# Zero fills and bands issued from SyncE, eight units of image 0 first, weights loaded one at a time, and a later second half of the reciprocal spread

## The chip, the cores and the metric

The kernel runs on one core of one Trainium2 chip. The metric is the device time in microseconds of one execution; the runs before the change took 3051.0, 3051.75 and 3055.79 us.

The engines are called as the profile calls them: PE (TensorE) with its weight loads PEld, DVE (VectorE), ACT (ScalarE), POOL (GpSimd), and SP (SyncE), which here only issues DMAs.

## The reference, cut to what matters

Two images of 256 channels and 64 x 64 pixels, all float32, pass two layers.

Layer 0 is attention over all 4096 pixels of an image, 8 heads of 32 channels: q, k and v are 1x1 convolutions, `softmax(q k / sqrt(32)) v` is concatenated to x and goes through a 1x1 convolution, and a mask resized from 32 x 32 blends the result with x.

Layer 1 multiplies by a channel gate (two small matmuls, sigmoid), does attention in windows of 8 x 8 pixels with 4 heads, adds, shuffles the channels, and ends with a spatial gate: two grouped 7 x 7 convolutions with batch norm between and after, and `x * sigmoid(y)`.

```
attn = softmax(einsum('bnd,bmd->bnm', q, k))
hybrid = conv1x1(concat([x, attn @ v]), Wf, bf);  x = hybrid*m + x*(1-m)
x = x * sigmoid(channel gate);  x = x + window_attention(x)
y = relu(bn1(conv7x7(x, sa_w1)));  y = bn2(conv7x7(y, sa_w2));  out = x * sigmoid(y)
```

## The kernel before, in words

**Preparation.** q, k and v of all pixels are computed and stored in DRAM. `prepare` readies the small tensors, among them a DRAM tile of zeros (`zero_s`) and the scaled filter rows `r1_s` and `r2_s`, from which the banded weight matrices of the 7 x 7 convolutions are made.

**Bands.** The convolutions run on PE as products with banded matrices, one per unit (`NU` = 16 units of four groups of channels), 896 KB each, in the DRAM tensor `w_s`. `bands()` is a generator that makes them by DMAs alone: 16 copies of `zero_s` into `w_s` (L341, DRAM to DRAM), then 156 copies that put filter rows on the diagonals (L349, L355, L362), each for all 16 units at once in pieces of 28 or 7 floats. Every `next` on it issues one DMA, and the loop calls it in every fifth slot (`i % 5 == 1`).

**The main loop.** It has 1024 slots: 2 images x 8 chunks of 512 queries x 2 head groups x 32 blocks of 128 keys; 64 slots make a chunk. Slot i computes the scores of slot i+2 on PE (`sa`, L632), whose exponentials go through ACT into one of `EB` = 8 buffers `ea` (L642), and the products of slot i with v (`ava`, L661). DVE adds the exponentials up for the denominators (`suma`, L663). Every four slots `load_piece` fetches k and v of a later piece (L559, L561) on SP, 256 KB each, into three buffers of each kind; such a load waits until PE is done with the piece whose buffer it takes[...].

**After a chunk.** Actions are queued with a delay in slots by `at`: `denominators` (`dna`) at DN = 8 slots after the chunk's last, the reciprocal one later, then `spread(0)` and `spread(1)` (`rda`, L699, each with an ACT copy, L706), the multiplication of `f` on DVE (L716), and the appending of `stage(b, c)`. `stage` is a generator with the rest of layers 0 and 1 for the chunk, from `hya` (L731) to the output projection `opa` (L952) and the addition into `xo` (L963), whose rows go to the DRAM tensor `x_s` (L978). It advances by one step in every fourth slot (`i % 4 == 0`), 13 calls in all.

**The convolutions** stand in another generator, `convolve`. It goes through `items`: a unit with image 0 alone, with image 1 alone, or with both. Units below `EARLY` are first done for image 0 alone, whose rows are all in DRAM by then. Item k is `conv1(k)` (`c1a`, L1043), `conv2(k)` (`c2a`, L1067) and `gate(k)` (`za`, L1089), which also stores the output (L1102); while item k is worked on, `conv1(k + 1)` goes ahead of `conv2(k)`. Each step ends in a `yield`. In the last chunk the loop starts the generator (first rows and unit 0's weights are loaded), and behind the last slot its steps are put between the steps of the last stage. When this stage is done, `staged` is set, and the rest of the items run alone: `more` gives out four tiles `xla` for rows of both images and loads the next four items' rows, which wait until the last `xs<-xo` stores have landed.

The weights of a unit (`wa<-ws`, L1015, 896 KB on SP) take the `e` buffers, of which there are 8. Units 1 to 8 are loaded at the generator's start, and the others, kept in `again`, one by one when a unit's buffer is free:

```
            for u in range(1, 1 + EB):
                load_w(u)
...
                if xcs or k + 4 < EARLY:
                    load_rows(k + 4)
                if (u >= 2) == (B - 1 in images) and u and again:
                    load_w(again.popleft())
```

Between `staged` and item `EARLY` the gates store on POOL alone; later on POOL and SP by turns.

Of the kernel before, what the change touches and what calls it, by code (L numbers as in the profile page):

```python
# [17 lines left out]
B, C, H, W = 2, 256, 64, 64  # L18
# [11 lines left out]
AHEAD = 2  # L30
EB = 8
DN = 8
EARLY = 7
HEADS1, HD1 = 4, 64
WS = 8
NW = W // WS
# [10 lines left out]
NU = NG // UG  # L47
# [8 lines left out]
def conv_seq_kernel(ctx: ExitStack, tc: tile.TileContext, a, out):  # L56
    nc = tc.nc
# [13 lines left out]
    def psum2(name):  # L71
        return ps["pair"].tile([P, 2, CH], F32, tag="s", name=name)
# [53 lines left out]
    w_s = dram.tile([NU, P, 2 * 32 * UW], F32, name="ws")  # L126
# [33 lines left out]
    zero_s = dram.tile([P, 2 * 32 * UW], F32, name="zeros")  # L160
# [171 lines left out]
    def spread(row, n):  # L332
        f = row.shape[-1]
        return row.rearrange("p u f -> u p f").to_broadcast([NU, n, f])


    def bands():
        band1 = w_s.rearrange("u p (m f) -> u (p m) f", f=UW)
        band2 = w_s.rearrange("u p (m f) -> u (p m) f", f=UW // 4)
        for u in range(NU):  # L340
            nc.gpsimd.dma_start(w_s[u], zero_s)  # L341
            yield
        for q in range(4):
            for dy in range(KS):
                r0, r1 = max(0, dy - PAD), min(RB, RB + dy - PAD)
                p0, m0, n = 32 * q + 1 + r0, 1 + r0 - dy + PAD, r1 - r0
                k = KS * q + dy
                at0, step = p0 * 64 + m0, 64 + 1
                nc.gpsimd.dma_start(  # L349
                    band1[:, at0 : at0 + step * (n - 1) + 1 : step, :], spread(r1_s[k : k + 1], n)  # L350
                )
                yield
                for i in range(4):
                    at0, step = p0 * 256 + 128 + i * 32 + m0, 256 + 1
                    nc.gpsimd.dma_start(  # L355
                        band2[:, at0 : at0 + step * (n - 1) + 1 : step, :],
                        spread(r2_s[k : k + 1, :, i], n),
                    )
                    yield
            for i in range(4):  # L360
                at0 = 32 * q * 256 + 128 + i * 32 + 1
                nc.gpsimd.dma_start(  # L362
                    band2[:, at0 : at0 + RB, :], spread(r2_s[32 + q : 33 + q, :, i], RB)
                )
                yield
# [157 lines left out]
    def pipeline(arm, shifted, pools):  # L523
# [23 lines left out]
        stages = deque()  # L547

        def at(delay, action):
            later.append((now[0] + delay, action))  # L550
# [99 lines left out]
        def products(i):  # L650
            b, c, g, m = slots[i]
            if m == 0:
                acc[0] = avp.tile([P, CH], F32, tag="av", name=f"av{arm}_{i}")
                acc[1] = ep.tile([P, HG, CH], F32, tag="sum", name=f"sum{arm}_{i}", bufs=3)
                totals[b, c, g] = acc[1]
            av, total = acc[0], acc[1]
            e, v = es[i], vts[b, c, g, m // PB]
            start, stop = m == 0, m == NMB - 1
            for j in range(HG):
                r = slice(32 * j, 32 * j + 32)  # L660
                nc.tensor.matmul(av[r, :], v[:, m % PB, r], e[:, j, :], start=start, stop=stop)  # L661
            if m > 0:
                nc.vector.tensor_add(total, first[0] if m == 1 else total, e)  # L663
            e = es.pop(i)
            if start:
                first[0] = e
            if stop:
                if g == 0:
                    fts[b, c] = fp.tile([P, KC, CH], F32, tag="f", name=f"f{arm}_{b}_{c}")
                f = fts[b, c]  # L670
                nc.scalar.copy(f[:, g, :], av)  # L671
                if g == 0:
                    return
                both = [totals.pop((b, c, gg)) for gg in range(KC)]
                inv = fp.tile([P, P], F32, tag="inv", name=f"inv{arm}_{i}")
                rd = fp.tile([P, KC, 4, P], F32, tag="rd", name=f"rd{arm}_{i}")


                def denominators():
                    s = psum2(f"dn{arm}_{i}")  # L680
                    for h in range(HEADS0):
                        for q in range(4):
                            r = slice(32 * q, 32 * q + 32)
                            nc.tensor.matmul(
                                s[r, 0, 0:P],
                                keysum[:, h].rearrange("p i h -> p (i h)"),
                                both[h // HG][:, h % HG, q * P : (q + 1) * P],
                                start=(h == 0),
                                stop=(h == HEADS0 - 1),
                            )  # L690
                    nc.scalar.copy(inv, s[:, 0, 0:P])


                def spread(hh):
                    t = psum2(f"rd{arm}_{i}_{hh}")
                    for gg in range(KC):
                        for q in range(2):
                            r = slice(64 * hh + 32 * q, 64 * hh + 32 * q + 32)
                            nc.tensor.matmul(  # L699
                                t[:, q, gg * P : gg * P + P],  # L700
                                spread_h[r, gg].rearrange("p j d -> p (j d)"),
                                inv[r, :],
                                start=True,
                                stop=True,
                            )
                    nc.scalar.copy(  # L706
                        rd[:, :, 2 * hh : 2 * hh + 2, :],
                        t[:, :, 0 : KC * P].rearrange("p q (g n) -> p g q n", g=KC),
                    )


                at(DN, denominators)
                at(DN + 1, lambda: nc.vector.reciprocal(inv, inv))
                at(DN + 2, lambda: spread(0))
                at(DN + 3, lambda: spread(1))
                at(DN + 4, lambda: nc.vector.tensor_mul(f, f, rd.rearrange("p g q n -> p g (q n)")))  # L716

# [271 lines left out]
        def convolve():  # L991
# [8 lines left out]
                nc.gpsimd.memset(t, 0.0)  # L1000
                ycs.append(t)
            xs, ws, ys = {}, {}, {}
            again = deque([*range(1 + EB, NU), 1])
            dst = out.rearrange("b (g i) r w -> b i r g w", i=4)

            def load_w(u):
                if u >= NU:
                    return
                n = 2 * 32 * UW
                if u == 0:  # L1010
                    t = cpool.tile([P, n], F32, name=f"w{arm}{u}")
                else:
                    t = ep.tile([P, HG, CH], F32, tag="e", name=f"w{arm}{u}")
                    t = t.rearrange("p h n -> p (h n)")[:, 0:n]
                nc.sync.dma_start(t, w_s[u])  # L1015
                ws[u] = t
# [103 lines left out]
            load_rows(3)  # L1120
            load_w(0)
            pool = yield
            for u in range(1, 1 + EB):
                load_w(u)
            conv1(0)
            yield
            for k, (u, images) in enumerate(items):
                while len(xs) <= k + 1 < len(items):
                    if not more():
                        yield  # L1130
                conv1(k + 1)
                yield
                more()
                z = conv2(k)
                yield
                more()
                gate(k, z)
                if xcs or k + 4 < EARLY:
                    load_rows(k + 4)

                if (u >= 2) == (B - 1 in images) and u and again:
                    load_w(again.popleft())

        def run_later():
            for _ in range(len(later)):
# [22 lines left out]
        for i, (b, c, g, m) in enumerate(slots):  # L1168
            now[0] = i
            if (b, c, g, m) == (B - 1, NCHUNK - 1, 0, 0):  # L1170
                for _ in banded:
                    pass
                conv = convolve()
                next(conv)
            if m % PB == 0:
                load_piece(i // PB + AHEAD)
            if g == KC - 1 and m == 0:
                nxt = (b, c + 1) if c + 1 < NCHUNK else (b + 1, 0)
                if nxt[0] < B:
                    load_q(*nxt)  # L1180
            rest = scores(i + 2) if i + 2 < len(slots) else None
            products(i)
            if rest:
                rest()
            if g == KC - 1 and m == NMB - 1:
                at(DN + 5, lambda b=b, c=c: stages.append(stage(b, c)))
            run_later()
            if i % 5 == 1:
                next(banded, None)
            if i % 4 == 0:  # L1190
                run_stages()
# [102 lines left out]
```

## Time and profile before

| what | value |
|---|---|
| median of 3 runs | 3051.75 us (3051.0 to 3055.79) |
| the profiled execution's own time | 3062.01 us |
| its span | 3060.2 us |
| mean granted PE clock | 0.987 |
| PE, DVE, ACT, POOL busy | 97%, 82%, 81%, 12% |
| DMA moved | 266.02 MB, mean 87 GB/s |

The profile is of one execution, which took 10 us more than the median run. Times in it count from the span's start. Some landmarks: the loop's first scores run at 187 us, the last ones at 2823 us, PE's last matmul ends near 3043 us. A row of a timeline gives the start, the time it takes, the engine, the line of the source, the operation, the tiles written and read, the number of instructions merged, and in brackets how long the engine stood idle before it and what ended this. "SPq" is SP's queue of DMA issues.

### The profile page before, as it was taken

How to read it: one execution, taken by the hardware profiler on the slowest of the kernel's cores; microseconds unless marked ns; L12 is line 12 of the kernel's file. 1: busy time of each engine (PE TensorE's matmuls, PEld its weight loads, DVE VectorE, ACT ScalarE, POOL GpSimd, SP SyncE). 2: the span in 40 equal slices, each digit the busy share in tenths (PEclk: the TensorE clock that was granted, in tenths of full speed). 3: DMA queues.
4: the chain of work that ended last, by engine and by line, in shares of the span. 5: the costliest groups of instructions: out<-in, count | busy, mean ns of one | idle time of the engine just before them, and what ended most of it. 6: DMA issues, size and time to landing. Idle time of an engine off the chain costs nothing.

```text
span 3060.2 us, 60785 instructions
## 1 busy us (share of the span) xinstructions
PE 2967.3 (97%) x25114; PEld 1005.6 (33%) x25114; DVE 2498.5 (82%) x1347; ACT 2478.7 (81%) x4147; POOL 369.4 (12%) x636
## 2 busy tenths in 40 slices
PE   9968989999999999999999999999999999999897
PEld 3541222222322222232222232322222322223675
DVE  3227989899989999899999898999999898999211
ACT  5537969898989899898989898989898898988333
POOL 8020000101010101010100101010101000000256
PEclk9988999999999999999999999999999999999999
DMA  8574212424252424243322314242424232423364
GB/s 241 200 248 106 63 52 60 71 63 73 60 78 60 70 70 73 67 66 75 63 65 64 68 60 73 62 71 60 69 71 71 66 71 66 102 63 101 96 208 112
DMA packets 155999, 266.02 MB, mean 87 GB/s; under 512 B 43016, under 2 KB 61756, under 8 KB 155456
## 3 DMA queue, kind: packets, MB, share of 16 engines
q1 hardware_dynamic: 127424, 213.86, 25.3%
q0 software_dynamic: 23728, 45.48, 9.8%
q8 instruction: 200, 3.28, 0.5%
q10 hardware_dynamic: 4560, 2.70, 0.3%
q14 instruction: 87, 0.71, 0.1%
HBM read 213.49 MB, written 66.13 MB: 91 GB/s over the span
## 4 chain that ended last, share of the span: by engine, by line
PE 71%; DVE 13%; DMA 4%; issue 2%; ACT 2%; POOL 1%; SPq 0%; DVEq 0%; ACTq 0%
PE sa L632 29%; PE ava L661 27%; DVE suma L663 11%; PE qka L802 4%; PE hya L731 4%; DMA ka<-ks 2%; PE vwa L888 2%; ACT ea L642 1%; PE opa L952 1%; PE c2a L1067 1%; POOL out_dram L1102 1%; DMA wa<-ws 1%; PE c1a L1043 1%; PE sca L836 1%; PE rda L699 1%
## 5 line engine op out<-in xcount | busy, mean ns | idle before, releaser
L663 DVE TENSOR_TENSOR suma<-suma,ea 128x2048 f32<-128x2048 f32 x960 | 2198.7, 2290 | 122.7 <-ACT ea L642 39.5
L642 ACT ACTIVATE ea<-sa 128x512 f32<-128x512 f32 (+1 forms) x3072 | 2043.7, 745 | 122.0 <-PE sa L632 75.4
L632 PE MATMUL sa<-qa,ka 32*128 32x512 f32 x8192 | 1186.6, 641 | 39.7 <-DMA ka<-ks 38.2
L661 PE MATMUL ava<-ea,va 128*32 128x512 f32 x8192 | 1093.8, 605 | 0.3 <-ACT fa L671 0.3
L632 PEld LDWEIGHTS sa<-qa,ka 32*128 32x128 f32 x8192 | 331.2, 183 | 793.6 <-ACT ea L642 688.7
L661 PEld LDWEIGHTS ava<-ea,va 128*32 128x32 f32 x8192 | 161.8, 108 | 781.9 <-issue 755.7
L978 POOL DMA_DIRECT2D xs<-xo x94 | 66.1, 711 | 2302.4 <-DVE xo L963 2302.2
L1102 POOL DMA_DIRECT2D out_dram<-za x204 | 114.9, 571 | 102.4 <-DVE za L1089 55.5
L802 PE MATMUL qka<-ua,qkv_w 128*128 128x512 f32 x256 | 118.4, 605 | 0.0
L663 DVE TENSOR_TENSOR suma<-ea,ea 128x2048 f32<-128x2048 f32 x32 | 73.1, 2285 | 51.3 <-ACT ea L642 51.3
L1089 DVE TENSOR_TENSOR za<-za,xla 128x1536 f32<-128x1536 f32 (+1 forms) x16 | 22.6, 1409 | 110.0 <-ACT za L1083 56.7
L453 DVE TENSOR_REDUCE top<-sq 128x512 f32<-128x2048 f32 x16 | 36.6, 2286 | 81.4 <-ACT sq L447 81.4
L739 ACT ACTIVATE ta<-hya,bf 128x512 f32<-128x512 f32 x32 | 20.3, 684 | 99.7 <-PE hya L731 99.7
L1067 PE MATMUL c2a<-yca,wa 32*128 32x192 f32 (+1 forms) x1288 | 95.9, 440 | 4.0 <-issue 3.8
L1077 ACT ACTIVATE za<-c2a 128x384 f32<-128x384 f32 (+1 forms) x46 | 25.8, 615 | 86.3 <-DMA out_dram<-za 50.2
L743 DVE TENSOR_TENSOR ta<-ta,mca 128x512 f32<-128x512 f32 x32 | 22.0, 689 | 88.3 <-ACT ta L739 88.3
L1067 PEld LDWEIGHTS c2a<-yca,wa 32*128 32x128 f32 x1288 | 87.0, 314 | 14.9 <-issue 14.0
L857 ACT ACTIVATE ewa<-ewa,mxwa 128x64 f32<-128x64 f32 x256 | 85.5, 362 | 1.5 <-DVE mxwa L848 1.5
L355 POOL DMA_DIRECT2D ws<-r2s x112 | 69.7, 625 | 95.3 <-DMA ws<-r2s 48.6
L815 ACT ACTIVATE qka<-qka,qkv_b 128x512 f32<-128x512 f32 x64 | 40.7, 695 | 41.6 <-PE qka L802 41.6
L802 PEld LDWEIGHTS qka<-ua,qkv_w 128*128 128x128 f32 x256 | 46.0, 189 | 71.3 <-issue 58.7
L434 PE MATMUL q<-x,WqT 128*128 128x512 f32 x128 | 62.2, 631 | 5.6 <-DMA WqT<-in_WqT_dram 5.6
(141 smaller groups left out, 1620.5 us busy)
## 6 DMA issues: line engine op xcount, KB each, us to landing
ka<-ks SPq DMA_DIRECT2D x256, 256.0 KB
va<-vs SPq DMA_DIRECT2D x256, 256.0 KB
wa<-ws SPq DMA_DIRECT2D x17, 896.0 KB
ws<-zeros POOLq DMA_DIRECT2D x16, 896.0 KB, 23.9
xs<-xo POOLq DMA_DIRECT2D x78, 140.0 KB, 8.0
xla<-xs SPq DMA_DIRECT2D x25, 420.0 KB
x<-in_x_dram SPq DMA_DIRECT2D x16, 512.0 KB
qs<-qst SPq DMA_DIRECT2D x16, 512.0 KB
```

The costliest lines, as they stand in the source:

```text
L355: nc.gpsimd.dma_start(band2[:, at0 : at0 + step * (n - 1) + 1 : step, :], spread(r2_s[k : k + 1, :, i], n),)
L434: nc.tensor.matmul(s[:, g, :], w[:, kc, g * P : (g + 1) * P], rhs, start=(kc == 0), stop=(kc == KC - 1),)
L632: nc.tensor.matmul(heads[j], k[r, cols], q[r, g, :], start=True, stop=not shifted)
L642: nc.scalar.activation(e[:, h, :], tile, AF.Exp, scale=SCALE0)
L661: nc.tensor.matmul(av[r, :], v[:, m % PB, r], e[:, j, :], start=start, stop=stop)
L663: nc.vector.tensor_add(total, first[0] if m == 1 else total, e)
L731: nc.tensor.matmul(s[:, oc, :], wf[:, kc, oc * P : (oc + 1) * P], f[:, kc - KC, :] if half else xw[kc], start=(kc == 0), stop=(kc == 2 * K ...
L802: nc.tensor.matmul(s[:, j, :], wqkv[:, kc, o : o + P], u[:, kc, :], start=(kc == 0), stop=(kc == KC - 1),)
L857: nc.scalar.activation(e[:, n, :], e[:, n, :], AF.Exp, bias=mx[:, n : n + 1], accum_out=rs[:, n : n + 1],)
L978: eng.dma_start(x_s[b, n, p + r0 : p + r1].rearrange("r g w -> g r w"), xo[64 * h : 64 * h + 64, oc, r0 - WS * c : r1 - WS * c, :],)
L1067: nc.tensor.matmul(tiles[j // 2][:, j % 2, 0 : n * W], w[r, d], y[r, 0:n, d : d + W], start=(d == 0), stop=(d == KS - 1),)
L1102: engines[stores % len(engines)].dma_start(dst[b, i, r0:r1, UG * u : UG * u + UG, :], z[p + r0 : p + r1, :, nb * m + n, :],)
```

## The change

1. `bands()` issues its 16 zero fills and 156 band copies on SP instead of POOL. Their place in the program's order is the same.
2. `EARLY` is 8 instead of 7: unit 7 is done for image 0 alone and later for image 1 alone, where one item did both. There are 24 items instead of 23.
3. At the convolutions' start only units 1 and 2 are loaded. The others follow one at a time behind the gates, in every item but item 7.
4. `spread(1)` comes one slot later than before, and so do the multiplication of `f` and the appending of the stage.

```
-EARLY = 7
+EARLY = 8
...
         for u in range(NU):
-            nc.gpsimd.dma_start(w_s[u], zero_s)
+            nc.sync.dma_start(w_s[u], zero_s)
             yield
...
-                nc.gpsimd.dma_start(
+                nc.sync.dma_start(
                     band1[:, at0 : at0 + step * (n - 1) + 1 : step, :], spread(r1_s[k : k + 1], n)
                 )
...
-                    nc.gpsimd.dma_start(
+                    nc.sync.dma_start(
                         band2[:, at0 : at0 + step * (n - 1) + 1 : step, :],
...
-                nc.gpsimd.dma_start(
+                nc.sync.dma_start(
                     band2[:, at0 : at0 + RB, :], spread(r2_s[32 + q : 33 + q, :, i], RB)
                 )
...
                 at(DN + 2, lambda: spread(0))
-                at(DN + 3, lambda: spread(1))
-                at(DN + 4, lambda: nc.vector.tensor_mul(f, f, rd.rearrange("p g q n -> p g (q n)")))
+                at(DN + 4, lambda: spread(1))
+                at(DN + 5, lambda: nc.vector.tensor_mul(f, f, rd.rearrange("p g q n -> p g (q n)")))
...
-            again = deque([*range(1 + EB, NU), 1])
+            weights = deque([*range(1, NU), 1])
...
-            for u in range(1, 1 + EB):
-                load_w(u)
+            for _ in range(2):
+                load_w(weights.popleft())
...
-                if (u >= 2) == (B - 1 in images) and u and again:
-                    load_w(again.popleft())
+                if weights and (k < EARLY - 1 or k >= EARLY):
+                    load_w(weights.popleft())
...
-                at(DN + 5, lambda b=b, c=c: stages.append(stage(b, c)))
+                at(DN + 6, lambda b=b, c=c: stages.append(stage(b, c)))
```

## The prediction

> **What bounds the kernel now.** I read the page first, then the timelines of the two places where TensorE is not full. The page:
>
> ```profile
> span 3060.2 us, 60785 instructions
> PE 2967.3 (97%) x25114; PEld 1005.6 (33%) x25114; DVE 2498.5 (82%) x1347; ACT 2478.7 (81%) x4147; POOL 369.4 (12%) x636
> PE   9968989999999999999999999999999999999897
> DMA  8574212424252424243322314242424232423364
> L663 DVE TENSOR_TENSOR suma<-suma,ea 128x2048 f32<-128x2048 f32 x960 | 2198.7, 2290 | 122.7 <-ACT ea L642 39.5
> L632 PE MATMUL sa<-qa,ka 32*128 32x512 f32 x8192 | 1186.6, 641 | 39.7 <-DMA ka<-ks 38.2
> ```
>
> PE is full except in the third slice and in the last tenth. L632 waited 39.7 us in all, 38.2 of it for k tiles: nearly one wait. The windows, cut from one `hya` to the next, show the loop between (columns: window, its length, busy time of PE, PEld, DVE, ACT, POOL with counts, clock, DMA share, GB/s):
>
> ```profile
> 735.55:899.50 163.95, 163.43 (x1369) 47.70 (x1369) 151.83 (x79) 145.21 (x247) 13.62 (x21) 1.00 0.36 68
> 2369.32:2532.50 163.18, 162.44 (x1369) 47.43 (x1369) 151.06 (x78) 145.12 (x247) 5.74 (x8) 1.00 0.27 68
> ```
>
> A chunk lasts 163.2 to 164.0 us and PE works through it: 64 slots of 2.07 us (scores 1.07, products 1.00) plus some 30 us of stage matmuls. DVE has 151 us, so it is second. Little is to be had there. Now the third slice, by the timelines of POOL, SP and PE:
>
> ```profile
> 189.56 3.40 POOL L341 DMA_DIRECT2D ws<-zeros  x7 [0.19 <-issue]
> ...
> 216.09 0.49 POOL L341 DMA_DIRECT2D ws<-zeros  x1 [2.87 <-DMA ws<-zeros]
> ```
>
> ```profile
> 192.12 0.43 SPq L559 DMA_DIRECT2D ka<-ks  x1
> ```
>
> ```profile
> 202.32 1.06 PE L661 MATMUL ava<-ea,va 128*32 128x512 f32 x8
> 241.08 2.09 PE L632 MATMUL sa<-qa,ka 32*128 32x512 f32 x8 [37.69 <-DMA ka<-ks]
> ```
>
> The program spaces the zeros five slots apart, but POOL has nothing else to wait for and issues all 16 (14.7 MB) in 28 us. The k tile issued on SP at 192.12 lands 48.8 us later. PE stands for 37.69 us, then runs two slots at a lower clock. Last, the tail on PE:
>
> ```profile
> 2833.75 2.65 PE L1067 MATMUL c2a<-yca,wa 32*128 32x192 f32 x40
> 2840.19 1.68 PE L1067 MATMUL c2a<-yca,wa 32*128 32x192 f32 x16 [3.79 <-issue]
> ...
> 2900.84 3.56 PE L1067 MATMUL c2a<-yca,wa 32*128 32x192 f32 x56
> 2908.44 4.72 PE L1043 MATMUL c1a<-xla,wa 128*32 128x192 f32 x56 [4.04 <-DMA xla<-xs]
> ```
>
> Two gaps, one in mid-tile where no operand is awaited, one for the rows of image 1 to come back from DRAM. After 2908.44 PE has no gap until its last matmul near 3043.
>
> [...]
>
> **Zeros on SP.** SP meets each zero in program order, between k and v loads that wait for PE to free buffers. So zeros go out one per five slots (10.4 us). Their transfer is about 3.1 us each (16 in some 50 us of the flood, 314 GB/s in that window), plus 512 KB of k and v per four slots: half of what the DMA engines moved in the flood. Gone: the gap, 37.7 us, and the slow slots (241.08 to 248.13 is 7.05 us for two slots, 2.9 over 4.14): 40.6 us. Given back: the pause had let DVE catch up. DVE needs 2.39 us a slot against PE's 2.07; 57 slots after the pause (score groups stretch from 1.14 to 1.46 us at 359.79) the eight `e` buffers are full and PE goes at 2.39 until the first stage. Those 57 slots now begin 8 earlier: 8 x 0.32 = 2.6 us. **Net -38.0 us.**
>
> **Bands on SP.** 156 more issues. SP's own rows bound one: 0.32 us (k) to 0.69 us (`xs<-xo`, 1.37 for two, as many short pieces). With zeros at 0.43 that is 57 to 115 us of SP, which waits 2,100 us for PE on the lines of k and v. Queued behind them are those loads, on which PE waits. Their lead: k issued at 251.45 is needed in slot 18, near 268.8, so 17 us; v (256.58) is alike. On the ring a band weighs little: DMA share is 0.36 in the window with 13 bands, 0.27 in the one with none, 0.09 x 163 / 13 = 1.1 us each. I take 0 us; the bound above is the rival D below, below it is nothing, as no wait on bands is on PE. POOL keeps the row stores, which nobody on the path waits for in the loop.
>
> **Spread.** `spread(1)` and the multiply move one slot, and the stage append too, from DN+5 to DN+6. Stages are advanced only in slots divisible by four, and the append fell on slot 12, so the stage now begins at slot 16. Same matmuls, copies and DMAs; its x and mask loads move along, with 48 slots still ahead of use. All waits of `rda` for the reciprocal after the first chunk come to 7.0 us, and they are on `spread(0)`, which stays. Bounds: -7 us (all gone) and +12 us (15 chunks at 164.0 instead of 163.2). I take 0. The last step of the stage of (1,6) now falls behind the slots: 1.3 us of DVE and four POOL stores (2.8 us), under `hya`.
>
> **Tail.** (1) At its start SP issues 8 weight loads of 0.92 MB (2814 to 2832); now 2. [...] Gone: 3.8 us, and the slow clock behind it (`hya` 6.02 against 3.70, `rda` 2.02 against 1.36, c2a's rest 0.6): 3.4 us. Together -7 us; 0 if the reading is wrong. (2) Weights 3 to 6 now go behind the output stores and rows of gates 0 to 3, in place of arriving early. Such loads took 5.4 to 7.6 us in the chain; unit 3 is issued near 2854 and wanted near 2859 on the earlier clock, 5 and 6 similar, 4 has room: +2 us (0 to 5). (3) Unit 7 is issued after gate(4). In SP's order the four `xla` loads stand ahead, and they wait for the row stores (issued at 2904.72). So the added item of image 0, meant for that round trip, waits for it too: 4 x 0.43 MB + 0.92 MB = 2.64 MB at 300 GB/s is 8.8 us, plus 2 us of latency, from an issue near 2904.7 - 5 = 2899.7. Its conv1 starts near 2910.5; before, the item at that place started at 2908.4. So the gap grows from 4 to 11 us, and items 1 and 2 are in this: **+2.1 us** in sum. (4) Unit 7 as two single items: a single takes 2.46 + 3.51 = 5.97, a double 4.75 + 4.89 = 9.64: **+2.3 us**. (5) Gates 4 to 7 store on POOL alone, 12 x 0.57 = 6.8 us per 6 us item: +0.5 us. Tail: **+5 us**.
>
> **Sum:** -38 + 5 = -33 us. The profiled execution took 3062.0 us (span 3060.2), so 3029. The median of the runs is 3051.75, 10.3 less, and I carry the difference over: **3019 us**.
>
> **Rivals.** B, the mid-tile gap is not of the weights: -33 + 7 = -26, 3026 us. For it: the profile says only "issue". C, unit 7 arrives in time (rows land sooner, or the loads overlap): -33 - 7 = -40, 3012 us. Against it: SP's order. D, slower: bands hold SP's ring. POOL's bands land in 9 to 20 us at the median; were this occupation and not latency, k would land after its 17 us of lead. It decides from 17.2 us on (156 x 0.2 us eats the gain); at 17.5, 156 x 0.5 - 33 = +45, 3097 us. Against it: 1.1 us by the DMA share. E, the flood only changes place: a zero is one large transfer and each k behind it is late by its rest, say 1.5 us for 16: the gain shrinks by 24, 3043 us. Against it: the lead of 17 us.
>
> **How the numbers follow.** Forecast A 0.62, B 0.17, C 0.11, E 0.05, D 0.05. A measurement tells 0.2% (6 us) from no change. Faster 0.94, same 0.02, slower 0.04. A's own spread is -34 to -42 for the zeros and 0 to +10 for the tail, 3010 to 3028; with B, C and the spread's bounds 3005 to 3036.
>
> **What would show it.** Right: `ws<-zeros` in SP's timeline some 10 us apart, L632's wait for `ka<-ks` near zero, the first `hya` some 30 us earlier (38 less four slots), chunks still at 163 us, no "issue" gap in the first c2a, and an 8th `xea` conv1 that waits some 11 us for `wa<-ws`. Wrong: new `ka` or `va` waits in the loop, chunks of 165 us, or a gap by the 8th item no longer than 4 us.

## The result and the profile after

The changed kernel takes 3021.31 us (3019.96 to 3021.95, four runs), the kernel before beside it 3053.71 us (3051.0 to 3055.79, four runs): a ratio of 0.9894, interval 0.9877 to 0.9911. The forecast was 3019 us, in a range of 3005 to 3036. The profiled execution after took 3021.93 us. Against the profiled one of before, the gain is 40.1 us; against the medians it is 32.4 us. That difference comes back below.

The lines of the page after that answer to those shown of before:

```profile
span 3020.1 us, 61026 instructions
PE 2970.8 (98%) x25226; PEld 1017.2 (34%) x25226; DVE 2503.1 (83%) x1348; ACT 2480.6 (82%) x4151; POOL 267.1 (9%) x470
PE   9999899999999999999999999999999999999897
DMA  8544322222142323232222222222323222321564
L664 DVE TENSOR_TENSOR suma<-suma,ea 128x2048 f32<-128x2048 f32 x960 | 2199.1, 2291 | 88.7 <-ACT ea L643 2.3
L633 PE MATMUL sa<-qa,ka 32*128 32x512 f32 x8192 | 1191.4, 640 | 1.5 <-ACT vst L480 1.2
```

The lines of the source stand one or two lower than before (L632 is L633, L1043 is L1045). PE's third slice is full, DMA's third slice went from 7 to 4, and the scores' idle time fell from 39.7 us to 1.5 us, none of it for k. POOL has 166 instructions fewer. SP's timeline shows where the zeros went:

```profile
193.76 0.59 SPq L342 DMA_DIRECT2D ws<-zeros  x1
194.50 0.46 SPq L560 DMA_DIRECT2D ka<-ks  x1
199.58 0.32 SPq L562 DMA_DIRECT2D va<-vs  x1
199.95 0.93 SPq L342 DMA_DIRECT2D ws<-zeros  x1
...
208.27 0.47 SPq L342 DMA_DIRECT2D ws<-zeros  x1
...
224.75 0.47 SPq L342 DMA_DIRECT2D ws<-zeros  x1
```

They leave in the program's order, 6 to 17 us apart, held by the loads of k and v around them: over the run SP waited 888.3 us for PE's `sa` at the k line and 1110.8 for its `ava` at the v line. The k issued at 194.50, right behind a zero, made nobody wait.

To see where the time went, I cut each span at the first `hya` (layer 0's fusion) of the first and of the fifteenth stage, both read from the chain of waits or PE's timeline. Between them lie 14 chunks. Each kernel's single profiled execution gives, in us:

| kernel | to the first hya | 14 chunks | from the 15th hya on |
|---|---|---|---|
| before | 408.38 | 2287.66 | 364.16 |
| after | 378.72 | 2280.05 | 361.33 |
| difference | -29.66 | -7.61 | -2.83 |
| with the stage's shift of four slots (8.3 us) put back | -38.0 | -7.6 | +5.5 |

The column on the right is called the rest below. The last row is needed because the later append starts every stage one step, four slots of 2.07 us, later: `hya` moves away from the start and nearer to the end, and no time is won by that. The sum had -38, 0 and +5. In the chain of waits after, the chunks run evenly:

```profile
704.44 7.06 PE hya L732 x16
...
867.30 7.06 PE hya L732 x16
...
1030.16 7.07 PE hya L732 x16
```

Each takes 162.86 us, where before they took 163.18 to 164.00. Last, the tail on PE:

```profile
2788.58 3.58 PE L1069 MATMUL c2a<-yca,wa 32*128 32x192 f32 x56
...
2839.46 4.19 PE L1045 MATMUL c1a<-xea,wa 128*32 128x192 f32 x56 [1.84 <-DMA wa<-ws]
...
2853.20 3.58 PE L1069 MATMUL c2a<-yca,wa 32*128 32x192 f32 x56
2866.15 4.62 PE L1045 MATMUL c1a<-xea,wa 128*32 128x192 f32 x56 [9.38 <-DMA wa<-ws]
```

The first c2a is one piece of 56 products, without the 3.79 us pause. The eighth item of image 0 waits 9.38 us for its weights (the sum had 11). SP's timeline shows unit 7's load behind the four `xla` loads:

```profile
2856.16 2.01 SPq L1024 DMA_DIRECT2D xla<-xs  x4
2858.22 1.54 SPq L1017 DMA_DIRECT2D wa<-ws  x3
```

### The profile page after: what moved, and what is told of

Its sections match the earlier page's. It is cut to its first block, busy times and chain, and to the rows that moved or that the text cites. A ratio compares the mean times of both kernels' runs of the same rounds, so it can differ in the third digit from the quotient of the medians.

```text
span 3020.1 us, 61026 instructions
## 1 busy us (share of the span) xinstructions
PE 2970.8 (98%) x25226; PEld 1017.2 (34%) x25226; DVE 2503.1 (83%) x1348; ACT 2480.6 (82%) x4151; POOL 267.1 (9%) x470
## 4 chain that ended last, share of the span: by engine, by line
PE 92%; DVE 2%; DMA 2%; POOL 1%; ACT 1%; issue 1%; SPq 0%; ACTq 0%; DVEq 0%; POOLq 0%
PE sa L633 36%; PE ava L662 33%; PE hya L732 4%; PE qka L803 4%; PE vwa L889 2%; PE opa L953 2%; PE v L472 2%; PE q L435 2%; PE k L435 2%; DVE suma L664 1%; POOL out_dram L1104 1%; PE c1a L1045 1%; PE c2a L1069 1%; DMA out_dram<-za 1%; PE dna L685 1%
## 5 line engine op out<-in xcount | busy, mean ns | idle before, releaser
L633 PE MATMUL sa<-qa,ka 32*128 32x512 f32 x8192 | 1191.4, 640 | 1.5 <-ACT vst L480 1.2
L633 PEld LDWEIGHTS sa<-qa,ka 32*128 32x128 f32 x8192 | 338.0, 183 | 755.4 <-ACT ea L643 688.3
L1091 DVE TENSOR_TENSOR za<-za,xla 128x768 f32<-128x768 f32 (+1 forms) x16 | 21.7, 1359 | 108.0 <-DMA out_dram<-za 57.9
L889 PE MATMUL vwa<-qkv_w,ua 128*128 128x256 f32 x256 | 59.5, 386 | 0.0
```

The source lines that it names most:

```text
L633: nc.tensor.matmul(heads[j], k[r, cols], q[r, g, :], start=True, stop=not shifted)
L889: nc.tensor.matmul(sv[:, t, :], u[:, kc, t * P : (t + 1) * P], wqkv[:, kc, 2 * C : 3 * C], start=(kc == 0), stop=(kc == KC - 1),)
```

## The experiments

Eleven kernels ran. Those of one comparison ran beside the same runs of the kernel before, whose median was 3060.34 us for the first four below (3057.0 to 3067.06), 3055.18 for e6 to e9 and 3055.27 for e5, e10 and e11; ratios are to these.

**The moved DMAs alone.** Kernel before, with the zeros and the bands' three lines on SP.

```
-            nc.gpsimd.dma_start(w_s[u], zero_s)
+            nc.sync.dma_start(w_s[u], zero_s)
...
-                nc.gpsimd.dma_start(
+                nc.sync.dma_start(
```

> The kernel before, with only the 16 zero fills and 156 band copies issued on SyncE. If the pause at the loop's start is the flood of zeros, as the prediction has it, the wait of L632 for ka<-ks goes from 38 us to under 2, the first hya comes 38 us earlier (near 370 us), the chunks after it stay at 163.2 to 164.0 us, and the time falls by 38 us. If the gap between the profiled execution and the median run (3062 against 3054) lies in that pause, the unprofiled time falls by 28 to 32 us only, to some 3023. The rival that band copies hold up k and v on SyncE's queue expects new waits for ka or va and chunks above 164 us.

3020.44 us (3018.89 to 3022.01), ratio 0.9867, 0.9853 to 0.9881. To the first `hya` 369.64 us, 38.7 less than before; the 14 chunks 2285.26, the rest 362.20. So the moved DMAs are the whole gain of the change, and the other two parts together add nothing: the profiled execution after is 3.0 us longer than e1's (3020.1 against 3017.1 us). The chunks of e1 are 2.4 us shorter than before's, without any change to the spread or the stage; e5 below shows why.

**The later spread and stage alone.** Kernel before, with

```
-                at(DN + 3, lambda: spread(1))
-                at(DN + 4, lambda: nc.vector.tensor_mul(...))
+                at(DN + 4, lambda: spread(1))
+                at(DN + 5, lambda: nc.vector.tensor_mul(...))
...
-                at(DN + 5, lambda b=b, c=c: stages.append(stage(b, c)))
+                at(DN + 6, lambda b=b, c=c: stages.append(stage(b, c)))
```

> The kernel before, with only the spread's second half, the multiplication and the stage moved by one slot. The prediction took 0 us. The profile of the changed kernel has chunks of 162.86 us where before had 163.18 to 164.00; over 14 chunks that is 7.6 us. If this part alone does it, the chunks are 162.9 us here too, the wait of rda for the reciprocal (7.0 us) is gone, and the time falls by 6 to 8 us. If the steadier chunks come from the POOL queue being free of bands, nothing changes here (under 2 us).

3057.42 us (3051.74 to 3062.3), ratio 0.9987, 0.9979 to 0.9994: 3 to 4 us, where 6 to 8 had been expected. Most of its profiled chunks take 162.86 us, but one takes 164.68 and one 170.35. In the longest POOL issues a burst of bands, and PE stops inside the products of one tile. PE's timeline shows the stop, and the windows what went on ahead of it (880 to 891) and around it (891 to 897; columns: window, length, busy time of PE, PEld, DVE, ACT, POOL with counts, clock, DMA share, GB/s):

```profile
891.46 1.05 PE L661 MATMUL ava<-ea,va 128*32 128x512 f32 x5
896.30 1.92 PE L661 MATMUL ava<-ea,va 128*32 128x512 f32 x3 [3.79 <-issue]
```

```profile
880.00:891.00 11.00, 11.00 (x144) 4.35 (x140) 10.69 (x6) 9.14 (x16) 3.10 (x5) 1.00 1.11 56
891.00:897.00 6.00, 2.21 (x14) 0.33 (x8) 5.69 (x4) 2.32 (x4) 0.62 (x1) 0.89 0.69 85
```

Ahead of the stop the DMA share is 1.11, at only 56 GB/s. By the trace's packets 0.58 of it is POOL's queue, which carries row stores and bands in short pieces. Around the stop itself the share is 0.69.

**The stage's append alone.** Kernel before, spread as it was.

```
-                at(DN + 5, lambda b=b, c=c: stages.append(stage(b, c)))
+                at(DN + 6, lambda b=b, c=c: stages.append(stage(b, c)))
```

> The kernel before, with only the stage appended one slot later (so that it starts at slot 16 of a chunk instead of 12); both spreads and the multiplication stay. Theory one: the stage's last big step, opa, now runs four slots nearer to the reciprocal, DVE has 4 x 0.32 us less arrears then, and the wait of rda for the reciprocal (0.74 us in 11 chunks) goes: 6 to 8 us as with the whole part. Theory two: the spacing of the two spreads is what helps (their two PSUM pairs and ACT copies no longer in consecutive slots): under 2 us here.

3048.54 us (3042.48 to 3055.11), ratio 0.9962, 0.9948 to 0.9975: 8.9 us faster than with the spread moved too. Its chunks take 162.66 us but for one of 164.39, which has a stop of 1.14 us in mid-tile. Its rest is 349.32 us: 14.8 less than before, 8.3 by the shift and 6.5 with the pause of the first c2a gone, though the eight weight loads are all still issued there. PE, SP and POOL in its timelines:

```profile
2824.39 3.58 PE L1067 MATMUL c2a<-yca,wa 32*128 32x192 f32 x56
```

```profile
2803.43 17.06 SPq L1015 DMA_DIRECT2D wa<-ws  x8
```

```profile
2832.87 2.77 POOL L978 DMA_DIRECT2D xs<-xo  x4 [168.63 <-DVE xo L963]
```

Before, the loads were issued from 2814.21, and POOL's row stores at 2824.60, nine microseconds ahead of the c2a. Here the stores come behind it. The windows around the c2a, of before and then of e4 (the last two columns are DMA share and GB/s):

```profile
2824.00:2833.00 9.00, 8.40 (x179) 6.55 (x175) 7.69 (x5) 2.99 (x6) 2.77 (x4) 1.00 1.04 255
2833.00:2841.50 8.50, 4.71 (x88) 4.27 (x79) 0.95 (x1) 0.27 (x1) 0.00 (x0) 0.80 0.94 306
```

```profile
2816.00:2824.00 8.00, 7.41 (x176) 6.43 (x174) 4.00 (x2) 1.64 (x4) 0.00 (x0) 1.00 0.97 377
2824.00:2830.00 6.00, 5.86 (x93) 5.02 (x83) 0.95 (x1) 2.23 (x5) 0.00 (x0) 1.00 0.24 95
```

With the stores among them the DMA engines moved 255 and 306 GB/s, at a share of 1.04 and, under the c2a, still 0.94. Without the stores they moved 377 GB/s ahead of the c2a, and under it their share was 0.24.

**The tail alone.** Kernel before, with the eighth unit and the weights one at a time.

```
-EARLY = 7
+EARLY = 8
...
-            for u in range(1, 1 + EB):
-                load_w(u)
+            for _ in range(2):
+                load_w(weights.popleft())
...
-                if (u >= 2) == (B - 1 in images) and u and again:
-                    load_w(again.popleft())
+                if weights and (k < EARLY - 1 or k >= EARLY):
+                    load_w(weights.popleft())
```

> The kernel before, with only EARLY = 8 and the weights loaded one at a time. The prediction's tail is +5 us: the mid-tile gap of c2a (3.8 us) and the slow clock after it gone (-7), small waits for weights (+2), the eighth item waiting some 9 to 11 us for unit 7's weights, one more single item (+2.3). So 2 to 8 us slower than before. If the mid-tile gap is not due to the eight loads, it is still there and the time is 10 to 14 us longer. The rival for this part, that the eighth item fills the round trip, expects 0 to 6 us less.

3069.3 us (3066.87 to 3073.37), ratio 1.0029, 1.0017 to 1.0040: slower by some 9 us, a little more than the 2 to 8 expected. The rest is 371.60 us, 7.4 more than before. The pause is gone here too, now with the row stores at their old time and two loads instead of eight, and the eighth item waits:

```profile
2831.22 3.58 PE L1067 MATMUL c2a<-yca,wa 32*128 32x192 f32 x56
...
2909.53 4.72 PE L1043 MATMUL c1a<-xea,wa 128*32 128x192 f32 x56 [11.07 <-DMA wa<-ws]
```

e3 and e4 together: here the pause came only with the eight loads and the row stores at once. Either part of the change removes it, so the two do not add.

**Which half of the tail costs.** The changed kernel with unit 7 loaded one place earlier (three ahead), with `EARLY` back at 7, or with eight ahead:

```
e6   -            for _ in range(2):
     +            for _ in range(3):
     -                if weights and (k < EARLY - 1 or k >= EARLY):
     +                if weights and (k < EARLY - 2 or k >= EARLY):
e7   -EARLY = 8
     +EARLY = 7
e8   -            for _ in range(2):
     +            for _ in range(8):
     -                if weights and (k < EARLY - 1 or k >= EARLY):
     +                if weights and (k == 1 or k >= EARLY):
```

> The changed kernel, with three units' weights loaded at the convolutions' start instead of two, so that each later unit goes one gate earlier and unit 7 stands ahead of the row loads that wait for the last stores (no load at items 6 and 7). If the 9.4 us wait of the eighth item is SyncE's order, it goes, with the slow clock behind it and the waits of 1.2 and 1.8 us: 12 to 16 us less than the changed kernel, near 3007. If the rows of image 1 are what ends the wait anyway, the ninth item waits in its place and the gain is under 6 us.

> The changed kernel with EARLY back at 7. Unit 7's weights are no longer wanted in the round trip: the first item of image 1 waits for its rows alone, some 4 us as in the kernel before, and one single item less saves 2.3 us. Expected 6 to 9 us less than the changed kernel, near 3014. If the ninth item's wait does not depend on EARLY, the time is within 3 us of the changed kernel.

> The changed kernel with all eight early units' weights loaded at the convolutions' start again. [...] it comes back (about 4 us idle and 3 us of slow clock), while the waits for wa<-ws (12.5 us and the slow clock behind) go: 6 to 9 us less than the changed kernel. If the gap had another cause, it stays away and the gain is 13 to 16 us, as with three ahead.

e6 3011.86 us (3010.23 to 3012.87), 0.9852, 0.9835 to 0.9868; e7 3011.44 (3010.08 to 3012.62), 0.9852, 0.9836 to 0.9869; e8 3009.18 (3008.44 to 3011.38), 0.9845, 0.9831 to 0.9860. The rests are 351.82, 349.80 and 349.96 us against 361.33 after. So the order of the loads and the eighth unit cost 10 to 12 us only together. With three ahead unit 7's load is no longer behind the rows, and the gap after the last early c2a is gone:

```profile
2854.57 3.58 PE L1069 MATMUL c2a<-yca,wa 32*128 32x192 f32 x56
2858.08 2.55 PE L1045 MATMUL c1a<-xla,wa 128*32 128x192 f32 x56
```

e6 saved 9.5 us where 12 to 16 had been expected. In e8 the pause was expected back, if it belonged to the eight loads; it did not come: the stage's shift had already moved the stores away from them (2797.64, behind the c2a at 2789.16). That miss agrees with the reading of e3 and e4 above.

**The zeros alone.** Kernel before, bands on POOL.

```
-            nc.gpsimd.dma_start(w_s[u], zero_s)
+            nc.sync.dma_start(w_s[u], zero_s)
```

> The kernel before, with only the 16 zero fills on SyncE; the band copies stay on GpSimd. If the fills are the whole of that part, the first hya is 38 us earlier and the time equals that with fills and bands on SyncE (3017 to 3023, within 2 us). The trace with spread and stage moved and the bands on GpSimd has, however, one chunk of 170.4 us, with a pause of 3.8 us between two matmuls of one tile while band copies ran in a burst behind the row stores. If such pauses belong to bands on GpSimd, this kernel has chunks above 163.5 us here and there, and lies 3 to 10 us above that one, with a wider spread over its runs.

3016.08 us (3013.04 to 3021.3), ratio 0.9869, 0.9854 to 0.9884, the same as e1 by the ratio. The 3 to 10 us above e1 did not come in the median, so the zeros carry the gain. The other two signs of bands on POOL came: the runs scatter over 8 us (e1's over 3), and the profiled execution, the longest of e5's four, has chunks of 164.33 and 165.06 us. Its 14 chunks take 2288.28 us, 3.0 more than e1's.

The traces say where such time goes. With bands on POOL (before, e2 to e5) the profiled loops have one or two stops each of 0.3 to 3.8 us in which PE waits for nothing that the profile shows, eight in all, besides the wait ahead of the first `rda`. With bands on SP (after, e1, e6 to e11) none has such a stop. So the bands too are better issued from SP, by 2.4 to 3.0 us in the traces (e1's chunks against before's and e5's), which is less than the runs can tell.

**The spread back, the stage late.** The changed kernel with

```
-                at(DN + 4, lambda: spread(1))
-                at(DN + 5, lambda: nc.vector.tensor_mul(...))
+                at(DN + 3, lambda: spread(1))
+                at(DN + 4, lambda: nc.vector.tensor_mul(...))
```

> The changed kernel with spread(1) and the multiplication back at DN+3 and DN+4; the stage stays at slot 16. If the second spread's place two slots behind the first costs 0.2 us a chunk (162.86 against 162.66), 2.8 us less than the changed kernel, 3017 to 3020. If the difference seen between those two kernels came with the bands on GpSimd, no difference here and chunks of 162.86.

3019.58 us (3018.7 to 3020.58), ratio 0.9885, 0.9869 to 0.9900. The chain's `hya` rows are 162.66 us apart, 0.2 us less than after:

```profile
704.23 7.06 PE hya L732 x16
...
866.89 7.06 PE hya L732 x16
...
1029.55 7.07 PE hya L732 x16
```

By the profiles the spread's delay costs 14 x 0.2 = 2.8 us, and e2 against e4 shows the same 0.2 us in most chunks. By the runs it is 1.7 us, with intervals that overlap. Between e2 and e4 the runs differ by 8.9 us, more than this term; both have bands on POOL and stops in the loop, and e2's profile has the long one.

**A later spread, and the best parts.** e10 is e1 (so `EARLY` = 7 and eight loads ahead) with the lines below. e9 is e6 with `spread(0)` at the same place, and `spread(1)` and the multiplication one slot later than in these lines.

```
-                at(DN + 2, lambda: spread(0))
-                at(DN + 3, lambda: spread(1))
-                at(DN + 4, lambda: nc.vector.tensor_mul(...))
+                at(DN + 4, lambda: spread(0))
+                at(DN + 5, lambda: spread(1))
+                at(DN + 6, lambda: nc.vector.tensor_mul(...))
...
-                at(DN + 5, lambda b=b, c=c: stages.append(stage(b, c)))
+                at(DN + 8, lambda b=b, c=c: stages.append(stage(b, c)))
```

> Three units' weights ahead, and besides both spreads, the multiplication and the appending of the stage two slots later (DN+4, DN+6, DN+7, DN+8), which still falls on slot 16 for the stage. In the changed kernel PE stands 9.0 us in the first chunk for the reciprocal, which DVE reaches late. With two slots of work put in between, the wait is 4 to 5 us shorter: 3 to 5 us less than with three ahead alone. If PE is then held up by the exponentials' buffers instead, there is no difference.

> The parts that paid, put together: fills and bands on SyncE; EARLY = 7 with eight units' weights ahead as in the kernel before; the stage at slot 16; and both spreads later but still in consecutive slots (DN+4 and DN+5, the multiplication at DN+6, the append at DN+8). Chunks of 162.66 us instead of 162.86 (14 x 0.2 = 2.8 us), a wait for the reciprocal in the first chunk 4 us shorter, and a tail of 349.3 us from the last-but-one hya instead of 361.3 (12 us): some 19 us below the changed kernel, 3000 to 3004. If the spacing of the spreads costs nothing, 3004 to 3008.

e9 3007.84 us (3005.84 to 3008.93), 0.9840, 0.9826 to 0.9854: 4 us below e6. Its profile has the first `hya` 3.9 us earlier (375.13 against 379.03). PE's waits show why: before the first `rda` PE waits 9.0 us in e6, and here, in e10's list (e9 has the same time):

```profile
PE rda L699 <- issue: 4.9, 1, 4.9
```

e10 3000.99 us (2999.92 to 3001.83), ratio 0.9822, 0.9809 to 0.9835: the fastest, 20 us below the changed kernel. It keeps the zeros and bands on SP and the later stage, leaves out the tail's part, and moves both spreads. Its chunks take 162.66 us, with `spread(1)` two slots later than before but next to `spread(0)`; e9's, with a slot left free between the two, take 162.87. So the 0.2 us are of the gap between the two spreads and not of the delay.

## Why the prediction held, and where it did not

**The zeros: right, and by the mechanism named.** 38.0 us forecast, 38.7 us measured by e1 to the first `hya`, 38.0 in the change itself with the shift put back. e5 shows that the zeros do it. The signs asked for came: zeros some 10 us apart, L632's wait for k gone, the first `hya` 29.7 us earlier.

**The bands: right that SP's queue bears them, and a little better than 0.** No wait for k or v appeared in the loop, neither after nor in e1, which refutes D and E. A k right behind a zero stayed inside its 17 us of lead: the one issued at 194.50 was not waited for. Not foreseen was that the bands cost something on POOL: the 2.4 us of the chunks between before and e1, by one execution each.

**The spread: wrong, a term of 0 that is some -5 us.** I argued that the 7.0 us of waits for the reciprocal stand before `spread(0)`, which stays where it is. They went all the same. Before and in e1 PE's waits have this row, here e1's; after, e4's and e11's lists have no such row:

```profile
PE rda L699 <- DVE inva L713: 8.9, 12, 0.7
```

The step that failed is the one that costed the moved append at nothing. The append alone takes 8.0 us from the 14 chunks (2285.26 in e1, 2277.26 in e11), and the gap between the spreads gives back 2.8 us: -5.2 us, in e1 against after. A reason for the first can be worked out, but no run isolates it: the reciprocal waits for DVE's arrears of sums, DVE loses 0.32 us on PE in every slot without stage work (2.39 against 2.07 us in before), and a stage that ends four slots nearer to the reciprocal leaves it, by estimate, 4 x 0.32 = 1.3 us less behind. Why the gap between the spreads costs 0.2 us a chunk is open.

**The tail: +5 forecast, +5.5 measured against before (+7.4 against e1, and +7.4 in e3), from terms that were each a little off.** (1) The pause with its slow clock (0.60 granted in before's 2843.6 to 2849.5): -7, measured -6.5 (e4). But it is not of the weights alone: here it came only with the row stores too, and the stage's shift alone removes it. The last section has more of it. Rival B was thus half right on the cause, and not on the sum. The pause is also not of one size: 3.79 us before, 2.38 in e1 and 2.97 in e5, at the same product, the 41st of 56, which is part of why the baselines differ. (2) Small waits for weights: +2, measured 1.24 and 1.84 us, and 1.65 for the slow group of 4.19 us behind the second, 4.7 us in sum. (3) The gap at the eighth item: +7 (4 to 11 us), measured 4.04 to 9.38, +5.3. The 300 GB/s and the 2 us of latency in its sum were estimates: in before the flood moved 314 GB/s, and a 16 KB store `out_dram<-za` landed 2.0 us after its issue at the median. (4) and (5): +2.8, and 5.5 + 6.5 - 4.7 - 5.3 = 2.0 is left for them. With the pause gone either way, the tail's part makes this kernel some 12 us longer: its rest is 361.33, against 349.32 in e4 with the tail of before.

**The carry-over: wrong by 9.7 us, and it hid the rest.** I took 10.3 us off the sum of 3029 because the profiled execution of before stood that far above the median. After, it stands 0.6 us above. By the profiles the change took 40.1 us where the sum had 33. The sum missed 7.1 us, and the chunks account for it with 7.6: -8.0 for the append, +2.8 for the gap between the spreads, -2.4 for the bands. These 7.1 us and the 9.7 us that the carry-over took too much cancel to 2.6. That the figure of 3019 came so close is luck, two errors of opposite sign; the loop's start, the larger part by far, was right by its mechanism. The medians of before lie between 3053.71 and 3060.34 us in the four comparisons, with runs from 3049.48 to 3067.06 us: beside the 23 runs around 3060.34 the profiled one, at 3062.01, is not a long one. What makes the comparisons differ is open.

## What to carry to other kernels

POOL, which waited for no other engine, issued the 16 zeros within 28 us, though the program has them five slots (10.4 us) apart. On SP's queue, which waits for the loop, they left 6 to 17 us apart, here at no cost, since the loads around them have 17 us of lead. Issue a weight that is wanted soon ahead of loads on its queue that wait for a round trip: here one place in the order was worth 9.5 us (e6). Measure the parts of a combined change one by one: one part here cost 10 to 12 us and was covered by another, and a version without it is 20 us faster.

## What the runs showed of the hardware

- PE stopped in mid-tile with no operand awaited. From 190 us on, and apart from the wait ahead of the first `rda` in every kernel, the traces have eleven such stops of over 0.3 us. Count PE's instructions (weight loads, matmuls and the waits among them): ten of the eleven come where the count leaves the same remainder by 256. Before's two lie 151 x 256 instructions apart, e2's two and the two longest of e5 97 x 256. In the six longest, of 1.21 to 3.79 us, a 16 KB packet of q8, the queue that the page calls "instruction", landed 1.39 to 1.50 us before PE went on. That PE waited for this packet fits these figures, but no run isolates it, nor what delayed the packet: the DMA share during the stop was 1.00 at 400 GB/s in before's c2a, 1.03 and 0.93 in e1's and e5's, and 0.74 in e2, behind 11 us at 1.11.
- The bytes moved didn't tell here how busy the DMA engines were: their share was 1.00 at 400 GB/s in before's tail, and 1.11 at only 56 GB/s in e2, under a burst of bands.
- A lower clock followed some short waits and not others. In the changed kernel a wait of 1.84 us was followed by a group of 4.19 us for 56 products that take 2.54 elsewhere (granted clock 0.58 in 2839.5 to 2843.6), and in e7 one of 2.18 us by 4.11. In e11 a wait of 1.88 us at the same place was followed by 2.53, and in e3 one of 1.78 by 2.54. Behind three longer waits the granted clock was lower too: before's of 37.69 us (0.56 in 241.0 to 248.2) and of 4.04 us (0.50 in 2908.4 to 2913.1), and the changed kernel's of 9.38 us (0.52 in 2866.15 to 2870.7).
- Kernels with bands on POOL scatter more: 5 to 13 us over the runs of before and of e2 to e5, against 2 to 3 us for after, e1 and e6 to e11. The former had 4 to 23 runs, the latter 4 or 5.
